# Three of four sums of the heads' outputs, moved one row later in the order of a two-layer attention kernel

## The chip, the cores and the metric

The kernel runs on one core of one Trainium2 chip. The metric is the device time of one execution in microseconds (us); before the change it is 1164.11, the median of three runs (1163.7 to 1166.31). Engines: TensorE (PE; PEld is its loading of stationary operands), VectorE (DVE), ScalarE (ACT), GpSimd (POOL) and SyncE (SP, which here only issues DMAs). Each works through its own queue in the order in which the program issued its instructions, and waits at semaphores for the others.

## The reference, cut to what matters

Two blocks follow one another on x of shape 2 x 1024 x 256 in float32: a one-head causal attention (hidden size 256) with layer norms, and then a second block, which takes most of the time: attention with 16 heads of 128, rotary positions and a causal mask, then a mixture of four experts with two chosen for each token.

```python
q = (h @ wq + bq).reshape(b, s, H, HD)...      # and k, v likewise
q = q * cos + _rotate_half(q) * sin            # and k
scores = jnp.where(causal, jnp.einsum('bhqd,bhkd->bhqk', q, k) / math.sqrt(HD), min)
out = jnp.einsum('bhqk,bhkd->bhqd', softmax(scores), v)
return out.transpose(0, 2, 1, 3).reshape(b, s, H * HD) @ wo + bo
```

The change lies in the second attention: between `out` of two heads and its product with `wo`.

## The kernel before, in words

**Units and rows.** The second attention goes head by head. A pair (g, b) is two heads (group g of 8) of batch element b; 16 pairs make 32 units of one head, and a unit has eight rows i = 0..7, each 128 queries against 128(i+1) keys. `RowB` (line 1123) has the steps of a row: `scores` on TensorE into a score tile of PSUM (two of these exist), then on VectorE `sc` minimum with the causal limit (L617) and the row's maximum (L619); `exponential` on ScalarE (L624); `normalise`, a reciprocal on VectorE (L1158) and a scaling on ScalarE (L1160); `transpose` on VectorE in 32 x 32 blocks (L662), two rows later; `gather`, sixteen DMAs on SP's queue for each four rows in two parts; and `output` on TensorE (L1209), which ScalarE moves into `aT_sb` (L1225). The output of rows 0 to 3 comes eight rows after row 3, that of rows 4 to 7 eight to ten rows after row 7.

**Seven pieces instead of eight.** While a pair's heads are worked through, the projections of the next pair's q and k and of its own v, and the output projection of the pair before, are done with seven half-size products instead of eight (Strassen's scheme in Winograd's form). A projection (`seven_products`, line 899) has pieces p1 to p7, called in the order p1, p2, p4, p3, p6, p5, p7. p2, p5 and p6 end with an addition on VectorE of a PSUM bank and a kept part (`summed`, L952); p7 ends on ScalarE (L944). p1, p3, p5 and p7 add up in one bank "a", so p7's products wait until p5's addition has read that bank. After p2, p6, p5 and p7 a rotation (`rotated`, line 827: two half multiplications L834, one multiplication L835, one addition L836, all on GpSimd) is queued for a later row. All VectorE additions of this kind read one operand from PSUM.

**The sums.** The seven pieces of the output projection (`seven_outputs`, line 1052) need four differences of the finished heads' outputs, `output_sums` (line 1045): each is one subtraction of 128 x 512 floats on VectorE (L1049) with both operands in SBUF.

```python
def output_sums(g, b, n):
    t1, t2, t4 = (scratch[:, ts(k, 512)] for k in range(3))
    b11, b12, b21, b22 = (output_block(g, b, j, k) for j in (1, 2) for k in (1, 2))
    out, in0, in1 = ((t1, b12, b11), (t2, b22, t1), (b12, b22, b12), (t4, b21, t2))[n]
    nc.vector.tensor_tensor(out, in0, in1, ALU.subtract)
```

Sum 0 gives t1, sum 1 t2, sum 2 overwrites b12, sum 3 gives t4. In this profile `scratch` has the name `we_flat`. The pieces are called by block and bank: 11a, 22c (uses t1), 11b, 12+a (t2), 12+c, 22+a (the new b12), 21+a (t4). Each is eight passes on TensorE (L1067) and an addition into `hx` on VectorE (L1076). 11a, 12+a, 22+a and 21+a share bank "a": each of the last three waits for the addition of the one before; 12+c follows 22c in bank "c" in the same way.

**The order.** A planner (`step`, line 1443) writes the calls of each row: scores, fills, exponential, output, mids, transpose of two rows earlier, normalise of one row earlier, gathers, ends, rotations. In the second head of a pair, rows 0 to 2 get two pieces of q each, row 3 gets p7, rows 4 to 6 two output pieces each and row 7 the last; `TS = (1, 2, 2, 3)` (line 1308) puts sum 0 into row 1, sums 1 and 2 into row 2 and sum 3 into row 3. Then `MOVES` (line 28), a list written out by hand, is applied to the names of the calls by `ordered` (line 302): each entry takes a call out and puts it right before another. The program is issued in the order that results; since every engine keeps its queue's order, that list decides what an engine does next. The output sums occur for 14 pairs: (0,0), (1,0), (1,1), (0,1), and (g, b) for g = 2, 3, 4 with both b, then (5,0), (5,1), (6,0), (7,0). They are named by the pair whose outputs are summed.

Of the kernel before, what the change touches and what calls it, by code (L numbers as in the profile page):

```python
# [78 lines left out]
    ("rotation 127", "RowB.normalise 251"),  # L79
    ("wq.7.1 p7", "wo.7.0 11a"),  # L80
    ("RowB.exponential 252", "wq.7.1 p7"),
    ("RowB.scores 252", "RowB.output 243 8"),
    ("RowB.transpose 249", "RowB.scores 252"),
    ("wq.7.1 p5", "RowB.gather 247 1"),
    ("RowB.normalise 250", "RowB.normalise 249"),
    ("rotation 125", "RowB.normalise 250"),
# [14 lines left out]
    ("RowB.gather 239 0", "RowB.normalise 241"),  # L101
    ("RowB.scores 242", "RowB.transpose 239"),
    ("wv.6.1 p3", "RowB.output 231 10"),
    ("wq.6.1 p3", "RowB.output 223 10"),
    ("RowB.normalise 227", "wv.7.0 p6"),
    ("RowB.exponential 227", "RowB.normalise 227"),
    ("RowB.scores 227", "RowB.exponential 227"),
    ("wq.7.0 p7", "weight_sums wv #8"),
    ("RowB.normalise 218", "output_sums 5 1 1"),
    ("RowB.exponential 218", "RowB.normalise 218"),  # L110
    ("wq.7.0 p3", "output_sums 5 1 0"),
    ("wq.7.0 p4", "wq.7.0 p3"),
    ("wv.6.0 p5", "RowB.gather 207 1"),
    ("RowB.scores 210", "RowB.gather 207 0"),
    ("RowB.transpose 202", "wq.6.0 p7"),
    ("RowB.normalise 202", "RowB.transpose 202"),
    ("RowB.transpose 201", "RowB.output 195 8"),
    ("rotation 102", "output_sums 5 0 3"),
    ("rotation 101", "rotation 102"),
    ("wq.6.0 p5", "rotation 101"),  # L120
    ("RowB.gather 199 0", "load_weights 6 wv"),
    ("RowB.transpose 199", "RowB.gather 199 0"),
    ("RowB.normalise 199", "RowB.transpose 199"),
# [1 line left out]
    ("output_weight_sums #7", "wv.5.1 p7"),  # L125
    ("RowB.scores 194", "RowB.gather 191 0"),
    ("wv.5.1 p3", "RowB.exponential 193"),
    ("wq.5.1 p3", "output_sums 4 1 0"),
    ("wq.5.1 p4", "wq.5.1 p3"),
    ("RowB.scores 178", "RowB.gather 175 0"),  # L130
    ("wv.5.0 p3", "RowB.exponential 177"),
    ("wo.4.0 12+a", "RowB.scores 173"),
    ("wo.4.0 11b", "wo.4.0 12+a"),
    ("RowB.exponential 174", "wq.5.0 p5"),
    ("RowB.scores 174", "RowB.exponential 174"),
    ("RowB.transpose 168", "RowB.scores 174"),
    ("rotation 83", "RowB.normalise 167"),
    ("output_weight_sums #6", "RowB.transpose 161"),
    ("RowB.normalise 161", "wv.4.1 p5"),
    ("wq.4.1 p3", "RowB.output 143 10"),  # L140
    ("wv.4.0 p3", "RowB.exponential 145"),
    ("wq.4.0 p3", "RowB.transpose 134"),
    ("wq.4.0 p4", "wq.4.0 p3"),
    ("RowB.normalise 131", "wv.3.1 p6"),
# [2 lines left out]
    ("output_weight_sums #5", "RowB.gather 127 0"),  # L147
    ("RowB.exponential 129", "wv.3.1 p4"),
    ("load_weights 4 wq", "load_weights 3 wo"),
    ("wq.3.1 p5", "RowB.gather 119 1"),  # L150
    ("RowB.exponential 127", "wq.3.1 p5"),
    ("RowB.scores 127", "RowB.exponential 127"),
# [3 lines left out]
    ("RowB.gather 111 1", "RowB.exponential 114"),  # L156
    ("RowB.scores 114", "RowB.transpose 111"),
    ("rotation 55", "wo.2.0 22c"),
    ("wq.3.0 p3", "RowB.output 95 10"),
    ("RowB.transpose 96", "wv.2.1 p5"),  # L160
    ("RowB.scores 98", "RowB.scores 97"),
# [2 lines left out]
    ("wv.2.1 p2", "wv.2.1 p4"),  # L164
    ("wv.2.1 p1", "wv.2.1 p2"),
    ("RowB.gather 91 1", "RowB.normalise 93"),
    ("RowB.transpose 89", "wq.2.1 p7"),
    ("wq.2.1 p5", "RowB.gather 87 1"),
    ("RowB.exponential 91", "wq.2.1 p6"),
    ("RowB.scores 91", "RowB.exponential 91"),  # L170
    ("RowB.scores 82", "RowB.gather 79 0"),
    ("wv.2.0 p3", "RowB.output 71 10"),
    ("RowB.transpose 72", "wq.2.0 p5"),
    ("RowB.exponential 75", "RowB.transpose 72"),
    ("RowB.scores 75", "RowB.exponential 75"),
    ("rotation 35", "RowB.normalise 71"),
    ("wv.0.1 p5", "RowB.gather 63 1"),
    ("wv.0.1 p2", "RowB.exponential 64"),
    ("wo.1.0 11a", "wo.1.0 22c"),
    ("wq.0.1 p7", "wo.1.0 11a"),  # L180
    ("wq.0.1 p5", "output_sums 1 0 3"),
    ("RowB.gather 55 1", "RowB.normalise 57"),
    ("weight_sums wv #2", "RowB.exponential 58"),
    ("RowB.exponential 49", "RowB.normalise 48"),
# [5 lines left out]
    ("RowB.transpose 43", "wo.0.0 12+a"),  # L190
    ("RowB.transpose 42", "wo.0.0 11b"),
    ("rotation 22", "weight_sums wk #2"),
    ("output_sums 0 0 3", "wq.1.1 p6"),
    ("output_sums 0 0 1", "RowB.scores 42"),
    ("RowB.transpose 39", "RowB.output 31 10"),
    ("RowB.transpose 38", "RowB.transpose 39"),
    ("wq.1.1 p4", "RowB.scores 41"),
# [1719 lines left out]
```

## Time and profile before

| | |
|---|---|
| time, median of 3 runs | 1164.11 us (1163.7 to 1166.31) |
| profiled execution: time, span from first to last instruction | 1165.19 us, 1163.4 us |
| mean granted TensorE clock | 0.994 |
| busy: PE, DVE, POOL, ACT | 1133.0, 852.5, 789.5, 648.7 us |
| L1049, output sums on VectorE | 56 instructions: 25.3 + 24.0 + 17.7 us busy |
| L952, the queries' additions (Twq) | 30 + 15 instructions, mean 680 and 678 ns |
| L1076, the output pieces' additions (hx) | 70 + 28 instructions, mean 680 and 682 ns |
| L834, L835, L836, rotations on GpSimd | means 1309/1300, 1341/1298, 1336/1281 ns |

A row of the profile's groups names the line, the engine, the operation, what it writes and reads, the count and the mean; a row of the timeline begins with the start and the duration in us. Numbers after `<-` in brackets are idle time of that engine and who ended it. The end of a matmul is modelled: a record of TensorE lasts longer than the distance to the next one's start, so the time that TensorE loses is read from the distances of starts.

### The profile page before, as it was taken

Reading aid. Unit: us, or ns where it says so; the run is one execution under the profiler, and the core shown is the slowest. Engines: PE = TensorE matmul, PEld = TensorE weight load, DVE = VectorE, ACT = ScalarE, POOL = GpSimd, SP = SyncE. Lnnn points to the kernel's source line nnn. Section 1 sums busy time; section 2 is a strip of 40 time slices with the busy share of each in tenths; the row PEclk is TensorE's granted clock in tenths of the full one; section 3 lists DMA queues with packets and bytes.
Section 4 is the critical chain, followed back from the end, with each engine's and each line's share of the span. In section 5 each row is a group of like instructions: output and inputs, shape, how many; then the busy total and the mean of one; then the engine's idle time right before and its main releaser. Section 6 shows DMA issues by size and latency. Waiting matters only on the chain.

```text
span 1163.4 us, 15802 instructions
## 1 busy us (share of the span) xinstructions
PE 1133.0 (97%) x4628; PEld 718.6 (62%) x4628; DVE 852.5 (73%) x1813; ACT 648.7 (56%) x1228; POOL 789.5 (68%) x749
## 2 busy tenths in 40 slices
PE   8999989999999999999999999999999999999997
PEld 5666636656565656565757475756566656566765
DVE  5667797868686868687877778777868677575675
ACT  3333676665656565656566656565565656553444
POOL 4005999989897979697878868797989897002100
PEclk9999999999999999999999999999999999899999
DMA  6132465665546454555555545564555657405011
GB/s 187 36 88 57 117 174 140 135 138 125 127 113 130 107 138 110 118 122 131 119 125 131 131 112 131 132 138 115 132 129 128 148 121 180 106 15 145 1 37 36
DMA packets 243221, 133.89 MB, mean 115 GB/s; under 512 B 18908, under 2 KB 241184, under 8 KB 242368
## 3 DMA queue, kind: packets, MB, share of 16 engines
q1 hardware_dynamic: 238096, 123.02, 45.6%
q0 software_dynamic: 1776, 4.89, 1.6%
q10 hardware_dynamic: 3264, 4.98, 1.2%
q8 instruction: 37, 0.61, 0.2%
q14 instruction: 48, 0.39, 0.1%
HBM read 22.71 MB, written 4.19 MB: 23 GB/s over the span
## 4 chain that ended last, share of the span: by engine, by line
PE 87%; DVE 8%; DMA 2%; issue 1%; SPq 1%; ACT 1%; POOL 0%; DVEq 0%; ACTq 0%; POOLq 0%
PE sc L1143 19%; PE av L1209 19%; PE pa L919 10%; PE pa L1067 5%; PE pa L910 5%; PE pa L1685 5%; PE pe L1708 4%; PE pc L919 4%; PE pa L741 2%; PE sc L692 2%; PE pc L1067 2%; PE pc L910 2%; PE pa L599 1%; PE pa L586 1%; PE pa L1019 1%
## 5 line engine op out<-in xcount | busy, mean ns | idle before, releaser
L1160 ACT ACTIVATE pr<-pr,rs 128x128 f32<-128x128 f32 (+3 forms) x252 | 195.6, 778 | 188.9 <-DVE rs L1158 188.9
L1143 PE MATMUL sc<-Twk,Twq 128*128 128x512 f32 (+3 forms) x768 | 289.5, 487 | 4.3 <-ACT pr L624 4.3
L624 ACT ACTIVATE pr<-sc,nmx 128x640 f32<-128x640 f32 (+7 forms) x272 | 200.9, 739 | 154.4 <-DVE nmx L619 121.6
L1209 PE MATMUL av<-pT,vg 128*128 128x512 f32 (+3 forms) x768 | 271.0, 490 | 4.7 <-DMA pT<-pair_sb 2.4
L834 POOL TENSOR_TENSOR rot<-Twk,rope_sb 64x512 f32<-64x512 f32 x128 | 167.6, 1309 | 92.2 <-DVE Twk L952 70.0
L1209 PEld LDWEIGHTS av<-pT,vg 128*128 128x128 f32 x768 | 143.5, 191 | 128.6 <-issue 99.3
L619 DVE TENSOR_REDUCE nmx<-sc 128x1 f32<-128x640 f32 (+7 forms) x272 | 206.1, 758 | 9.4
L1143 PEld LDWEIGHTS sc<-Twk,Twq 128*128 128x128 f32 x768 | 135.6, 191 | 123.9 <-issue 108.7
L834 POOL TENSOR_TENSOR rot<-Twq,rope_sb 64x512 f32<-64x512 f32 x128 | 166.3, 1300 | 8.8
L617 DVE TENSOR_TENSOR sc<-sc,limit 128x128 f32<-128x128 f32 x272 | 79.2, 291 | 99.6 <-PE sc L1143 84.0
L662 DVE STREAM_TRANSPOSE x<-pr 128x640 f32<-128x640 f32 (+1 forms) x124 | 128.4, 1036 | 19.6 <-ACT pr L1160 11.9
L835 POOL TENSOR_TENSOR Twk<-Twk,rope_sb 128x512 f32<-128x512 f32 x64 | 85.8, 1341 | 5.0
L836 POOL TENSOR_TENSOR Twk<-Twk,rot 128x512 f32<-128x512 f32 x64 | 85.5, 1336 | 5.0
L835 POOL TENSOR_TENSOR Twq<-Twq,rope_sb 128x512 f32<-128x512 f32 x64 | 83.1, 1298 | 5.0
L836 POOL TENSOR_TENSOR Twq<-Twq,rot 128x512 f32<-128x512 f32 x64 | 82.0, 1281 | 5.0
L1577 POOL TENSOR_TENSOR hx<-hx,x 128x256 f32<-128x256 f32 x16 | 11.5, 745 | 90.1 <-DVE hx L1717 82.7
L662 DVE STREAM_TRANSPOSE pair_sb<-pr 128x128 f32<-128x128 f32 (+1 forms) x120 | 60.2, 502 | 8.0 <-ACT pr L1160 7.8
L1685 PE MATMUL pa<-xT,we_flat 128*128 128x512 f32 x128 | 59.6, 611 | 0.8 <-DVE hx L1029 0.8
L1076 DVE TENSOR_TENSOR hx<-hx,pa 128x512 f32<-128x512 f32 x70 | 46.6, 680 | 13.6 <-PE pa L1067 13.5
L1225 ACT ACTIVATE aT_sb<-av,par 128x512 f32<-128x512 f32 x64 | 43.8, 684 | 21.3 <-PE av L1209 19.8
L1708 PE MATMUL pe<-lent,hT 128*128 128x256 f32 x240 | 54.2, 379 | 0.0
L624 ACT ACTIVATION_READ_ACCUMULATOR pr<-sc,nmx 128x1 f32 x272 | 53.4, 196 | 0.0
(215 smaller groups left out, 1810.5 us busy)
## 6 DMA issues: line engine op xcount, KB each, us to landing
pT<-x SPq DMA_DIRECT2D x496, 128.0 KB, 2.7
pT<-pair_sb SPq DMA_DIRECT2D x480, 64.0 KB, 2.0
pT<-aT_sb SPq DMA_DIRECT2D x48, 128.0 KB, 2.7
pT<-za SPq DMA_DIRECT2D x48, 64.0 KB, 2.1
wk_g<-in_L_ffn_wk_dram SPq DMA_DIRECT2D x9, 256.0 KB, 3.0
wq_g<-in_L_ffn_wq_dram SPq DMA_DIRECT2D x9, 256.0 KB, 3.1
wv_g<-in_L_ffn_wv_dram SPq DMA_DIRECT2D x9, 256.0 KB, 3.1
wo_g<-in_L_ffn_wo_dram SPq DMA_DIRECT2D x9, 256.0 KB, 2.9
```

Of the source, the lines that this page charges most:

```text
L619: nc.vector.tensor_reduce(nmx, sc[:, :L], AX.X, ALU.max, negate=True)
L624: nc.scalar.activation(pr[:, :L], sc[:, :L], AF.Exp, bias=nmx, accum_out=sm)
L662: nc.vector.transpose(z[:, i % 4, :n, :], pr[:, : n * 32].rearrange("p (m s) -> p m s", s=32))
L834: nc.gpsimd.tensor_tensor(rot[lo, :], t[hi, cs], rope_sb[hi, 1, cs], ALU.mult)
L835: eng.tensor_tensor(t[:, cs], t[:, cs], rope_sb[:, 0, cs], ALU.mult)
L836: nc.gpsimd.tensor_tensor(t[:, cs], t[:, cs], rot, ALU.add)
L919: nc.tensor.matmul(pa, lhsT=w, rhs=x, start=start, stop=True, skip_group_check=True)
L1143: nc.tensor.matmul(sc[:, ds(n0, n)], lhsT=qT[:, ts(i, P)], rhs=kT[:, ds(n0, n)], start=True, stop=True,)
L1160: nc.scalar.activation(self.pr[:, :L], self.pr[:, :L], AF.Copy, scale=rs)
L1209: nc.tensor.matmul(cut(av), lhsT=vg[g, b][:, c, ts(hh, HD)], rhs=cut(pT[:, c, :]), start=(c == 0), stop=(c == i),)
L1685: nc.tensor.matmul(ph, lhsT=we1_sb[:, e, c, ts(m, P)], rhs=x2T[:, c, ds(k0 * P, 512)], start=(c == 0), stop=(c == DC - 1),)
L1708: nc.tensor.matmul(pe[:, ts(n, D)], lhsT=hTs[b, j, e][:, c, ts(k, P)], rhs=we2_sb[e][:, c, :], start=(c == 0), stop=(c == IC - 1),)
```

## The change

The list of moves gets new entries. Sums 1 and 2 go from row 2 of the second head to row 3, right behind the row's scores, minimum and maximum; sum 3 goes from row 3 to row 4, at the same place in it. Sum 0 stays. Other new or altered entries only keep the calls around the sums where they were, since old entries had used a sum as their mark. What is computed is the same. The lines removed and added, in order:

```diff
-    ("RowB.scores 252", "RowB.output 243 8"),
+    ("RowB.scores 252", "output_sums 7 0 3"),
...
+    ("RowB.exponential 251", "RowB.transpose 249"),
+    ("output_sums 7 0 2", "RowB.exponential 251"),
+    ("output_sums 7 0 1", "output_sums 7 0 2"),
...
+    ("output_sums 6 0 3", "weight_sums wv #9"),
+    ("output_sums 6 0 2", "RowB.exponential 235"),
+    ("output_sums 6 0 1", "output_sums 6 0 2"),
...
-    ("RowB.normalise 218", "output_sums 5 1 1"),
+    ("output_sums 5 1 3", "wq.7.0 p7"),
+    ("output_sums 5 1 2", "RowB.exponential 219"),
+    ("output_sums 5 1 1", "output_sums 5 1 2"),
+    ("RowB.normalise 218", "wq.7.0 p6"),
...
+    ("output_sums 5 0 3", "weight_sums wv #7"),
...
-    ("rotation 102", "output_sums 5 0 3"),
+    ("rotation 102", "RowB.exponential 203"),
...
+    ("output_sums 5 0 2", "wq.6.0 p5"),
+    ("output_sums 5 0 1", "output_sums 5 0 2"),
...
+    ("output_sums 4 1 3", "wo.4.1 11a"),
+    ("output_sums 4 1 2", "RowB.exponential 187"),
+    ("output_sums 4 1 1", "output_sums 4 1 2"),
...
+    ("output_sums 4 0 3", "weight_sums wv #6"),
+    ("output_sums 4 0 2", "RowB.exponential 171"),
+    ("output_sums 4 0 1", "output_sums 4 0 2"),
...
+    ("output_sums 3 1 3", "wo.3.1 11a"),
+    ("output_sums 3 1 2", "RowB.exponential 155"),
+    ("output_sums 3 1 1", "output_sums 3 1 2"),
...
+    ("output_sums 3 0 3", "weight_sums wv #5"),
+    ("output_sums 3 0 2", "RowB.exponential 139"),
+    ("output_sums 3 0 1", "output_sums 3 0 2"),
...
+    ("output_sums 2 1 3", "wo.2.1 11a"),
+    ("output_sums 2 1 2", "RowB.exponential 123"),
+    ("output_sums 2 1 1", "output_sums 2 1 2"),
...
+    ("output_sums 2 0 3", "weight_sums wv #4"),
+    ("output_sums 2 0 2", "RowB.exponential 107"),
+    ("output_sums 2 0 1", "output_sums 2 0 2"),
...
+    ("output_sums 0 1 3", "wo.0.1 11a"),
...
-    ("RowB.scores 91", "RowB.exponential 91"),
+    ("RowB.scores 91", "output_sums 0 1 1"),
...
+    ("output_sums 1 1 3", "weight_sums wv #3"),
...
-    ("RowB.scores 75", "RowB.exponential 75"),
+    ("RowB.scores 75", "output_sums 1 1 1"),
+    ("RowB.exponential 74", "RowB.scores 75"),
+    ("wq.2.0 p6", "RowB.exponential 74"),
...
-    ("wq.0.1 p5", "output_sums 1 0 3"),
+    ("output_sums 1 0 3", "weight_sums wk #3"),
+    ("wq.0.1 p5", "RowB.exponential 59"),
+    ("output_sums 1 0 2", "wq.0.1 p5"),
+    ("output_sums 1 0 1", "output_sums 1 0 2"),
...
-    ("output_sums 0 0 3", "wq.1.1 p6"),
-    ("output_sums 0 0 1", "RowB.scores 42"),
+    ("output_sums 0 0 3", "wo.0.0 11a"),
+    ("output_sums 0 0 2", "RowB.exponential 43"),
+    ("output_sums 0 0 1", "output_sums 0 0 2"),
```

## The prediction

> **What bounds the kernel now.** I read the page first, then busy time in the stretch that the change touches, then the waits, then the rows of the moved sums, and last the timelines of one place. The page's engine shares and its chain:
>
> ```profile
> PE 1133.0 (97%) x4628; PEld 718.6 (62%) x4628; DVE 852.5 (73%) x1813; ACT 648.7 (56%) x1228; POOL 789.5 (68%) x749
> ...
> PE 87%; DVE 8%; DMA 2%; issue 1%; SPq 1%; ACT 1%; POOL 0%; DVEq 0%; ACTq 0%; POOLq 0%
> ```
>
> TensorE carries the chain. The windows view of 190 to 930 us, which holds thirteen of the fourteen places that change (the last lies at 944):
>
> ```profile
> 190.00:930.00 740.00, 734.09 (x3091) 457.79 (x3090) 563.79 (x1105) 443.42 (x843) 628.77 (x586) 1.00 0.55 127
> ```
>
> PE busy comes first: 5.9 us of 740 idle, at a granted clock of 1.00. Only TensorE's own waits can be won. The waits view of the same stretch has them:
>
> ```profile
> PEld pa L919 <- DVE Twq L952: 8.1, 12, 1.6
> ...
> PE pa L919 <- DVE Twq L952: 5.9, 7, 1.4
> ```
>
> Both are one wait: the queries' last piece p7 adds into the bank that p5's addition (L952, on VectorE) must first have read. In TensorE's timeline a 512-column pass starts every 0.43 us; what p7's first pass loses beyond its pitch is, by place (named by the pair whose outputs are summed): (0,0) 0.88, (1,0) 0.88, (1,1) 1.52, (0,1) 1.62, (2,0) 0.41, (2,1) 0.14, (3,0) 0.13, (3,1) 0.14, (4,0) 0.19, (4,1) 0.13, (5,0) 1.34, (5,1) 0.41, (6,0) 0.14, (7,0) none: 7.9 us. After each wait p7's second pass starts 0.10 late too: 13 x 0.10 = 1.3. So 9.3 us at most (more than the idle time, since a pass's record, 0.59, is longer than its pitch). The moved sums themselves, by their line:
>
> ```profile
> L1049 DVE TENSOR_TENSOR we_flat<-aT_sb,we_flat x28: 681/820/1751, 210.3 to 952.1; 128x512 f32<-128x512 f32 x28
> L1049 DVE TENSOR_TENSOR we_flat<-aT_sb x14: 681/1266/1567, 198.9 to 944.1; 128x512 f32<-128x512 f32 x14
> L1049 DVE TENSOR_TENSOR aT_sb<-aT_sb x14: 1298/1750/1756, 212.1 to 948.0; 128x512 f32<-128x512 f32 x14
> ```
>
> One shape takes from 681 to 1756 ns. Why, the timelines of VectorE and of GpSimd at (3,1) show:
>
> ```profile
> 606.34 0.56 DVE L619 TENSOR_REDUCE nmx<-sc 128x1 f32<-128x384 f32 x1
> 606.81 0.93 DVE L1049 TENSOR_TENSOR we_flat<-aT_sb,we_flat 128x512 f32<-128x512 f32 x1
> 607.66 1.75 DVE L1049 TENSOR_TENSOR aT_sb<-aT_sb 128x512 f32<-128x512 f32 x1
> 609.34 0.68 DVE L952 TENSOR_TENSOR Twq<-pc,part 128x512 f32<-128x512 f32 x1
> 609.94 0.68 DVE L952 TENSOR_TENSOR Twq<-pa,part 128x512 f32<-128x512 f32 x1
> ...
> 611.72 0.72 DVE L1049 TENSOR_TENSOR we_flat<-aT_sb,we_flat 128x512 f32<-128x512 f32 x1
> ...
> 613.99 0.68 DVE L1076 TENSOR_TENSOR hx<-hx,pa 128x512 f32<-128x512 f32 x1
> ```
>
> ```profile
> 607.27 1.60 POOL L835 TENSOR_TENSOR Twk<-Twk,rope_sb 128x512 f32<-128x512 f32 x1
> 608.95 1.60 POOL L836 TENSOR_TENSOR Twk<-Twk,rot 128x512 f32<-128x512 f32 x1
> 610.63 2.94 POOL L834 TENSOR_TENSOR rot<-Twq,rope_sb 64x512 f32<-64x512 f32 x2
> ```
>
> Sums 1 and 2 (606.81, 607.66) stand ahead of the additions of p6 and p5 (609.34, 609.94), whose pieces were done by 607.68. A sum ends 0.55 us after the GpSimd operation that it met: sum 2 at 609.41, that operation at 608.87. GpSimd's next one then takes 1.60 instead of 1.27. Sum 3 (611.72) met the last 0.17 us of an operation and took 0.72.
>
> **The change, part by part.** Applying both lists of moves to the sequence of calls, only the 42 sums change place; no instruction is added, no DMA moves. Sums 1 and 2 go behind the minimum and maximum of row i=3, sum 3 behind those of row i=4. Ahead of p5's addition they are gone at (0,0), (2,0) to (4,1), (5,1), (6,0) and (7,0), not at (1,0), (1,1), (5,0), where p5 follows row 3's scores, nor at (0,1), where both p6 and p5 do. Behind them now stand the transpose of row 1 and reciprocal of row 2, and behind sum 3 all four additions of the outputs' pieces (L1076); TensorE waits for those: 12+a for 11a's, 22+a for 12+a's, 21+a for 22+a's. In the trace these have 2.02, 1.50 and 2.40 us to spare, but at (0,0) 22+a has 0.44; at (2,1) 21+a has 0.69; at (4,0) 12+a has 0.93; at (5,1) 12+a has 1.19 and 22+a 0.96.
>
> What a sum costs at its new place no row shows. Bounds: 0.68 (no operation met) and 1.75 (a whole one). I take the end of the operation that it will meet plus 0.55. This is where a rule weighs against the change. The row: sum 3 took 0.68 to 0.72 at thirteen places, and at that price nine places just lose their waits. The Trainium skill, page "SBUF — State Buffer", section "Who interferes with whom", says that a VectorE instruction with two SBUF inputs and a GpSimd instruction that reads SBUF exclude each other, whoever starts first keeping the port to its end. Then 0.72 belongs to the old place, not to the sum. The rows of 1.75 behind another sum agree, so I follow the rule.
>
> Worked at (3,1); VectorE starts the next instruction some 0.08 before the last one's end. p6's addition at 606.87, p5's at 607.71 (its piece ends 607.68), transpose and reciprocal 0.27, row 3's minimum 0.30 and maximum 0.61 from 608.58: sum 1 starts at 609.49. GpSimd, undisturbed, runs 607.27 to 608.54 and 608.62 to 609.89 (1.27 each): sum 1 ends 610.44, the operation behind it takes 1.60 to 611.57, sum 2 ends 612.12. Transpose and reciprocal 0.42; row 4's scores end at 612.63 on a TensorE that is 0.24 ahead, so its minimum starts 612.66 (before 612.91) and sum 3 at 613.70. It meets an operation that ends at 614.60: 1.45 us. 11a's addition starts 615.07 (before 613.99); 12+a has 0.68 left. 12+a's addition ends 619.27; 22+a stands at 619.72: 0.45 left. By the addition of 21+a, where VectorE was idle for 1.05, it has caught up. Gain 0.24. Covers: ScalarE's exponential of row 3 comes earlier (609.6, before 611.9), that of row 4 as before; row 3's transpose, hence its gather on SP, is about 1.2 later, but is read eight rows on, over 20 us away, and its sixteen DMA issues take some 11 us. GpSimd is delayed by as many sums as before. Without the cover of those 0.45 us every late microsecond of VectorE is one of TensorE.
>
> The other places in the same way, minus is gain:
> - (3,0), (3,1), (4,1), (6,0): 0.23 + 0.24 + 0.24 + 0.24 = -0.95.
> - (2,0): -0.52, with 0.1 left at 22+a.
> - (0,0): -0.98; 12+a's addition ends 225.5 (before 225.2) with TensorE 0.98 ahead and 0.44 to spare: 22+a waits 0.88 + 0.10. Net 0.
> - (2,1): -0.24; sum 3 ends at 506.3, 11a's addition at 506.9, 12+a stands there at 506.64: +0.36; 22+a +0.25; 21+a +0.6. Net +1.0.
> - (5,1): -0.52; sum 3 ends 841.0, so 12+a waits 0.8 and 22+a 0.24. Net +0.5.
> - (4,0): -0.30 against +0.37 at 12+a, about 0. (7,0): no wait before, 0.8 left after, 0.
> - p5 still behind: (1,0) -0.43 and (1,1) -0.14, since the sums meet shorter remainders there; (0,1) +0.5, since sum 1 meets a longer one (1.5 instead of 1.09); (5,0): sum 1 and a GpSimd operation are ready at the same time, 776.17: -0.34 or +0.92, taken at +0.3.
>
> Sum: -0.95 - 0.52 + 1.0 + 0.5 - 0.43 - 0.14 + 0.5 + 0.3 = +0.3 us. On the profiled execution (1165.19; span 1163.4 and 1.8 around it) that makes 1165.5; it ran 1.08 above the median, 1164.11, so I predict 1164.4. The bounds: with every sum at 0.68 the nine freed places give -3.5, and at the other four VectorE saves 1.3 to 1.8 ahead of p5, which takes (1,0) -0.98, (1,1) and (0,1) -1.48 each, (5,0) -1.33: -8.8. With every sum at 1.75 it is +8.5 (rival b at all its places).
>
> **The rivals.**
> (a) The sums keep their prices, sum 3 at 0.72: nine waits vanish and nothing takes their place. 0.98 + 0.52 + 0.24 + 0.23 + 0.24 + 0.30 + 0.24 + 0.52 + 0.24 = 3.5: 1160.6. For it: VectorE is only 76% busy in the stretch (563.79 of 740), and its idle time grows when it needn't hold TensorE. Against: the spread of the sums' rows.
> (b) Slower: VectorE's backlog lands on the outputs' additions. If sum 1 meets a whole operation too (1.75 instead of 0.95) and sum 3 as well (1.75 instead of 1.45), 11a's addition comes 1.1 later still: at (3,1) 12+a then waits 1.1 - 0.68 = 0.42 and 0.10, and 22+a 1.1 - 0.52 - 0.45 = 0.13 and 0.10, in all 0.75 on top of my value. At half of the eleven places other than (1,0), (1,1), (7,0) that is +4.1, with my +0.3: 1168.5. It decides from the point where these additions come over 1.5 us later against TensorE than before. For it: GpSimd runs without a pause there (gaps of 0.08), and (0,0), (2,1), (4,0), (5,1) have less to spare. Against: a sum's mean meeting is half an operation.
> (c) The sums meet no operation of GpSimd: -8.8, so 1155.3. Against it: GpSimd's timeline has no gap for them, and sum 2, straight behind sum 1, took 1.75 at all but one place.
>
> **How the numbers follow.** Chances: the exchange 0.44 (own range 1162 to 1166.5), (a) 0.26 (1158.5 to 1161.8), (b) 0.27 (1166.5 to 1172), (c) 0.03. About 0.2% (2.3 us) is what a measurement can tell from no change. Of the exchange 0.40 lies within it and 0.02 at either side; (a) and (c) add 0.29 below, (b) 0.27 above: faster 0.31, same 0.40, slower 0.29. The range for 8 in 10 runs from 1159 to 1170; it leaves out (c) and the outer parts of (a) and (b).
>
> **What would show it.** Right: L919's wait for L952 under 0.1 at the regular places, but still over 0.4 at (1,0), (1,1), (0,1), (5,0); sum 3 mostly at 1.2 to 1.75 us; new waits of TensorE at L1067 for "DVE hx" at (0,0), (2,1), (5,1), together 2 to 4 us. Wrong towards (a): no such rows and a sum 3 near 0.7. Wrong towards (b): L1067 waits at most places. What would upset the working most is the phase of GpSimd's operations, which sets each sum's length and which I carried on from the old trace.

## The result

The changed kernel took 1166.37 us (median of 22 runs, 1162.96 to 1171.09), the kernel before 1163.21 us in the same set of runs (22, 1159.25 to 1166.95). The ratio is 1.0031, 95% interval [1.0019, 1.0042]: slower by 3.6 us, where +0.3 was predicted as the likeliest. The time lies inside the range, but on the far side of the 0.2% that I took for no change.

The profiled execution of after doesn't show this loss: 1165.7 us, span 1163.1, at a clock of 0.996 (before: 1165.19, 1163.4, 0.994). One profile is one draw: before's has one stretch more at half clock, behind a wait for a gather near 933 us. So the time is taken apart in two ways: TensorE's records of after and before (4628 each, in the same order), aligned one to one, give what each place gains or loses; the mean granted clock of all timed runs gives the rest. From after's page:

```profile
PE 1130.3 (97%) x4628; PEld 717.3 (62%) x4628; DVE 861.8 (74%) x1813; ACT 652.6 (56%) x1228; POOL 790.8 (68%) x749
```

VectorE is busy 9.3 us more for the same 1813 instructions. The line of the sums (L1087, before L1049) says where (minimum, median, maximum in ns):

```profile
L1087 DVE TENSOR_TENSOR we_flat<-aT_sb,we_flat x28: 681/1410/1741, 214.0 to 952.4; 128x512 f32<-128x512 f32 x28
```

This row holds sums 1 and 3; its median went from 820 to 1410. Sum 3 alone took 0.68 to 0.72 at thirteen places before and now takes 1.39 to 1.74 at twelve of fourteen. TensorE's own waits from 190 to 930 us (engine, line, whom it waited for; total us, times, longest):

```profile
PE pa L957 <- DVE Twq L990: 5.4, 4, 2.1
PE sc L1181 <- ACT pr L662: 0.9, 1, 0.9
PE pa L1105 <- DVE rs L1196: 0.6, 1, 0.6
PE pa L1105 <- DVE hx L1114: 0.6, 1, 0.6
```

Before, one row stood here: 5.9 us in 7 waits for p5's addition. Four are left, and they are longer (2.1 instead of 1.4); the three rows below are new. By place (what TensorE loses or wins there in all, in us; minus is gain):

| place | predicted | measured | what is seen in after |
|---|---|---|---|
| (3,0), (3,1), (4,1), (6,0) | -0.95 | -0.93 | no wait left |
| (2,0) | -0.52 | -0.51 | no wait left |
| (1,0), (1,1) | -0.57 | -0.57 | p7 waits 0.45, 1.38 |
| (0,0) | 0 | +0.11 | p7's wait gone, 0.3 at 12+a, 0.8 at 22+a |
| (0,1) | +0.5 | +0.41 | p7 waits 2.02 |
| (5,1) | +0.5 | +0.54 | 0.8 at 12+a, 0.2 at 22+a |
| (2,1) | +1.0 | +1.34 | 0.3 at 12+a, 1.2 at the scores |
| (4,0) | 0 | +0.29 | 0.2 at 11a, 0.4 at 12+a |
| (5,0) | +0.3 | +0.91 | p7 waits 2.25 |
| (7,0) | 0 | 0.00 | none within the place |
| sum | +0.26 | +1.59 | |

These 1.59 us are at full clock. The rest goes with the clock: the timed runs of after have a mean granted clock of 0.9946 (standard error 0.0003), those of before 0.9961, 0.9962, 0.9968 and 0.9973 in four later sets of runs; before's clock in the set of the result itself isn't on record. 0.001 of the clock is 1.2 us if TensorE is busy all the while (1160 us x 0.001). Over the 144 runs of before the span falls by 0.9 us for each 0.001, over after's 22 by 1.2. So a clock that is lower by 0.0015 to 0.0027 stands for 1.3 to 3.1 us. Together 2.9 to 4.7, against 3.6 [2.2, 4.9] measured. In the records, a stretch of reduced clock is 3.4 or 6.8 us at one half, so at most 1.7 or 3.4 us are lost. The stretch that ends every run (1.5 to 4.6 us of it within the span) finds TensorE idle: it counts in the mean clock and costs no time. Span times clock, roughly a run's time at full clock, has a mean of 1158.67 us in after, of 1157.18 in the 70 runs of before in the first two sets of experiments and of 1156.92 in all 144: +1.5 to +1.75, which agrees with the +1.59 of the aligned records.

**The worked place, (3,1).** VectorE and GpSimd in after:

```profile
607.84 0.69 DVE L990 TENSOR_TENSOR Twq<-pa,part 128x512 f32<-128x512 f32 x1 [0.17 <-PE pa L957]
...
609.63 0.87 DVE L1087 TENSOR_TENSOR we_flat<-aT_sb,we_flat 128x512 f32<-128x512 f32 x1
...
613.80 1.40 DVE L1087 TENSOR_TENSOR we_flat<-aT_sb,we_flat 128x512 f32<-128x512 f32 x1
615.12 0.68 DVE L1114 TENSOR_TENSOR hx<-hx,pa 128x512 f32<-128x512 f32 x1
```

```profile
608.68 1.27 POOL L874 TENSOR_TENSOR Twk<-Twk,rot 128x512 f32<-128x512 f32 x1
...
613.38 1.27 POOL L873 TENSOR_TENSOR Twq<-Twq,rope_sb 128x512 f32<-128x512 f32 x1
```

p5's addition now waits for TensorE (0.17) instead of TensorE for it. Sum 1 ends at 610.50, 0.55 after the GpSimd operation it met (609.95); sum 3 at 615.20, 0.55 after its one (614.65). The forecast had 610.44, and 615.15 for sum 3; 11a's addition was put at 615.07 and started at 615.12. The wait of p7 left and the sums paid for it on VectorE, as worked. The same holds far beyond this place: in all fourteen profiles (before, after and the twelve experiments) 780 of the 784 sums last 0.68 us or the rest of the GpSimd operation that they meet plus 0.55, whichever is longer, to 0.01 us; the other four are told in the last section.

### The profile page after: what moved, and what is told of

It is laid out like the page before. It is cut to its first block, busy times and chain, and to the rows that moved or that the text cites. A ratio compares the mean times of both kernels' runs of the same rounds, so it can differ in the third digit from the quotient of the medians.

```text
span 1163.1 us, 15808 instructions
## 1 busy us (share of the span) xinstructions
PE 1130.3 (97%) x4628; PEld 717.3 (62%) x4628; DVE 861.8 (74%) x1813; ACT 652.6 (56%) x1228; POOL 790.8 (68%) x749
## 4 chain that ended last, share of the span: by engine, by line
PE 85%; DVE 9%; DMA 3%; SPq 2%; issue 1%; ACT 0%; ACTq 0%; DVEq 0%
PE av L1247 19%; PE sc L1181 18%; PE pa L957 10%; PE pa L948 5%; PE pa L1723 5%; PE pa L1105 5%; PE pe L1746 4%; PE pc L957 4%; PE sc L730 2%; PE pc L948 2%; PE pa L779 2%; PE pc L1105 2%; SPq L711 2%; DMA pT<-x 2%; DVE we_flat L1087 1%; DVE nmx L657 1%
## 5 line engine op out<-in xcount | busy, mean ns | idle before, releaser
L1181 PE MATMUL sc<-Twk,Twq 128*128 128x512 f32 (+3 forms) x768 | 289.7, 487 | 5.3 <-ACT pr L662 5.3
L1181 PEld LDWEIGHTS sc<-Twk,Twq 128*128 128x128 f32 x768 | 135.6, 191 | 125.1 <-issue 109.3
L872 POOL TENSOR_TENSOR rot<-Twq,rope_sb 64x512 f32<-64x512 f32 x128 | 171.4, 1339 | 8.8
L874 POOL TENSOR_TENSOR Twk<-Twk,rot 128x512 f32<-128x512 f32 x64 | 82.5, 1289 | 5.0
L873 POOL TENSOR_TENSOR Twk<-Twk,rope_sb 128x512 f32<-128x512 f32 x64 | 82.0, 1281 | 5.0
```

What stands on the lines that cost most here:

```text
L872: nc.gpsimd.tensor_tensor(rot[lo, :], t[hi, cs], rope_sb[hi, 1, cs], ALU.mult)
L873: eng.tensor_tensor(t[:, cs], t[:, cs], rope_sb[:, 0, cs], ALU.mult)
L874: nc.gpsimd.tensor_tensor(t[:, cs], t[:, cs], rot, ALU.add)
L1181: nc.tensor.matmul(sc[:, ds(n0, n)], lhsT=qT[:, ts(i, P)], rhs=kT[:, ds(n0, n)], start=True, stop=True,)
```

## The experiments

**Theory.** An exchange, place by place: a sum is as long as what is left of the GpSimd operation it meets, plus 0.55 us. Where sums 1 and 2 are put behind p5's addition, p7's wait goes; where they stay ahead of it, it may grow; sum 3 in row 4 delays the output pieces' additions. **Rival A** for the rest of the loss: the two long waits, 2.0 us at (0,1) and 2.2 at (5,0), lower the clock. **Rival B**: the late stretch behind (7,0), where TensorE waits for gathers, does. A third possibility was that the exchange isn't what decides, but the mere length of the sums.

The edits are entries at the end of the list of moves, so each is shown by its pattern. "Clock" is the mean of the timed runs of the kernel, minus that of before in the same set of runs, with a standard error of 0.0004 to 0.0006 (0.0007 to 0.0009 where only five or six runs were timed); 0.001 is about 1 us.

| kernel | ratio [95%] | sum of places, us | clock, minus before's |
|---|---|---|---|
| seven places | 0.9985 [0.9975, 0.9996] | -2.0 | +0.0005 |
| four places | 1.0052 [1.0038, 1.0067] | +3.2 | -0.0016 |
| sum 3 late | 0.9990 [0.9978, 1.0002] | -1.85 | -0.0010 |
| p5 first | 0.9986 [0.9975, 0.9997] | -3.7 | -0.0018 |
| (7,0) alone | 1.0011 [0.9999, 1.0022] | +0.4 | -0.0012 |
| (0,1) and (5,0) alone | 1.0005 [0.9993, 1.0017] | +1.35 | +0.0004 |
| both, without (7,0) | 0.9910 [0.9891, 0.9928] | -8.03 | +0.0011 |
| both, with (7,0) | 0.9908 [0.9888, 0.9928] | -8.03 | +0.0013 |
| change without (7,0) | 1.0004 [0.9991, 1.0018] | +1.37 | +0.0002 |
| (7,0), sum 3 alone | 0.9999 [0.9986, 1.0011] | 0.0 | 0.0000 |
| (7,0), sums 1 and 2 alone | 1.0023 [1.0013, 1.0032] | +1.1 | -0.0012 |
| change, experts' loads late | 1.0040 [1.0025, 1.0056] | +1.63 | -0.0025 |

"Sum of places" leaves out the time lost to half clock inside a place (2.58 - 0.9 = 1.7 us at (5,0) in one profile, about as much at (0,1) in another).

**1. The change only where a gain was worked out.** On the kernel before:

```diff
+    ("output_sums 3 1 1", "RowB.exponential 155"),
+    ("output_sums 3 1 2", "RowB.exponential 155"),
+    ("output_sums 3 1 3", "wo.3.1 11a"),
...
```

and so at (1,0), (1,1), (2,0), (3,0), (4,1), (6,0).

> The change at seven places only: (1,0), (1,1), (2,0), (3,0), (3,1), (4,1), (6,0). Theory (the waits for p5 are exchanged, place by place, for sums that meet GpSimd operations and for waits of the outputs' pieces): these seven are the gaining ones, TensorE ends each of them earlier by 0.43, 0.14, 0.51 and four times 0.23, in all 2.0 us, as in the trace of the whole change; about 1161 us, ratio 0.998. Rival (the loss comes from later gathers behind the late transposes, whichever place is changed): TensorE's DMA waits behind the places grow and the ratio is above 1.

Measured 0.9985, -1.7 us; the seven places gave -0.41, -0.14, -0.51, -0.22, -0.24, -0.23, -0.24. **2. Only where a loss was worked out**, in the same way at (0,1), (2,1), (5,0), (5,1).

> The change at four places only: (0,1), (2,1), (5,0), (5,1). Theory: these lose, by 0.41, 1.34, 0.90 and 0.54, in all 3.2 us, so about 1166.4, ratio 1.003, as much as the whole change loses in its timed runs. Rival (the loss lies at the DMA waits near 990 us, made by the last places (6,0) and (7,0), which are unchanged here): no loss, 1163.

Measured 1.0052, +6 us in 5 runs, nearly twice what was expected; the places lost 0.43, 1.35, 0.9 and 0.53 at full clock, 3.2 in all. The rest goes with a lower clock (-0.0016, standard error 0.0008), here with (7,0) untouched; the profile has one stretch of half clock behind the wait at (5,0). So the change is a mixture of places with both signs, and at full clock its places add up: what each loses or gains alone, it does in the whole.

**3. Sum 3 later.** On the changed kernel, sum 3 at all fourteen places behind the addition of 22+a:

```diff
+    ("output_sums 3 1 3", "RowB.transpose 156"),
...
```

> The whole change, but sum 3 of all 14 places goes two rows later still, behind the addition of 22+a in row 6 (only 21+a in row 7 reads it). Theory: sum 3's 1.4 to 1.7 us ahead of 11a's addition is what makes 12+a and 22+a wait; moved behind them, (2,1), (5,1), (0,0) and (4,0) lose no time there, about 3 us under the whole change: 1163, unless 21+a at (2,1), where row 7 has no scores, waits up to 1 us. Rival (the sums 1 and 2 alone fill VectorE): the waits of 12+a and 22+a stay, 1166.

Measured 0.9990. (0,0) went from +0.11 to -0.84, (2,1) from +1.34 to +0.35, (4,0) from +0.29 to -0.13, (5,1) from +0.54 to -0.51, which are the places where sum 3 had eaten the slack of the output pieces. (0,1) and (5,0) stayed (2.08, of which some 1.7 half clock, and 0.90).

**4. Sums behind p5.** On the changed kernel, sums 1 and 2 behind p5's addition where that stands behind row 3's scores:

```diff
+    ("output_sums 1 0 1", "RowB.exponential 59"),
+    ("output_sums 1 0 2", "RowB.exponential 59"),
+    ("output_sums 1 1 1", "RowB.normalise 73"),
+    ("output_sums 1 1 2", "RowB.normalise 73"),
+    ("output_sums 0 1 1", "RowB.gather 87 1"),
+    ("output_sums 0 1 2", "RowB.gather 87 1"),
+    ("output_sums 5 0 1", "rotation 101"),
+    ("output_sums 5 0 2", "rotation 101"),
```

> The whole change, but at (1,0), (1,1), (0,1) and (5,0) sums 1 and 2 stand behind p5's addition instead of ahead of it. Theory: p7's waits there (0.45, 1.38, 2.02, 2.25 and 0.10 after each) go, 6.5 us under the whole change if the outputs' pieces there have the slack that the other places have, about 1160. Rival (VectorE's backlog only moves on): 12+a and 22+a wait there instead, at least half is given back, 1163 or more.

Measured 0.9986: (1,0) -0.57, (1,1) -1.62, (0,1) -1.68, (5,0) -0.62, where the change had -0.43, -0.14, +0.41, +0.91. VectorE's timeline at (5,0) in after:

```profile
776.13 1.72 DVE L1087 TENSOR_TENSOR we_flat<-aT_sb,we_flat 128x512 f32<-128x512 f32 x1
777.77 1.75 DVE L1087 TENSOR_TENSOR aT_sb<-aT_sb 128x512 f32<-128x512 f32 x1
779.44 0.68 DVE L990 TENSOR_TENSOR Twq<-pa,part 128x512 f32<-128x512 f32 x1
```

and GpSimd's at the same time:

```profile
776.04 1.27 POOL L874 TENSOR_TENSOR Twk<-Twk,rot 128x512 f32<-128x512 f32 x1
```

GpSimd started at 776.04, sum 1 at 776.13: 0.09 us too late, so it had a whole operation ahead of it, and p5's addition stood behind 3.3 us of sums. It fell so in all six profiles that have this order, by 0.08 to 0.11 us.

**5 and 6. Rivals A and B alone.** On the kernel before, the change only at (7,0), and only at (0,1) and (5,0):

```diff
+    ("output_sums 7 0 1", "RowB.exponential 251"),
+    ("output_sums 7 0 2", "RowB.exponential 251"),
+    ("output_sums 7 0 3", "RowB.output 243 8"),
```

```diff
+    ("output_sums 0 1 1", "RowB.exponential 91"),
+    ("output_sums 0 1 2", "RowB.exponential 91"),
+    ("output_sums 0 1 3", "wo.0.1 11a"),
+    ("output_sums 5 0 1", "wq.6.0 p5"),
+    ("output_sums 5 0 2", "wq.6.0 p5"),
+    ("output_sums 5 0 3", "weight_sums wv #7"),
```

> The change at (7,0) only. So far the places' own losses explain 1.6 us of the whole change, its timed runs lose over 3, and they show a lower granted clock (mean 0.9946 against 0.9967 before; one less in a thousand is 2.3 us at half clock and 1.2 us lost). Theory A (the clock drops after the long waits for p5, which are above 2 us at (0,1) and (5,0) only): here no place loses and the clock is as before, 1162.8 us, ratio 1.000, clock 0.997. Theory B (the clock drops at the gather waits near 933 and 990 us, which the last place (7,0) alone can disturb): clock 0.995 and 2 to 3 us more, ratio 1.002.

> The change at (0,1) and (5,0) only, where sums 1 and 2 stay ahead of p5. The places themselves lose 0.4 + 0.9 = 1.3 us. Theory A (waits over 2 us for p5 drop the clock): besides, the clock is lower in the mean, 0.995, and the time is some 3.5 us above before, ratio 1.003. Theory B (the gather waits behind (7,0) drop it): clock 0.997, 1.3 us more, ratio 1.001.

(7,0) alone: 1.0011, with an interval that just includes no change, and a clock lower by 0.0012 (1.1 to 1.4 us), though its records hold only a wait of 0.3 us and its echo of 0.1 at 955 us. (0,1) and (5,0) alone: 1.35 us of places and a clock as before. A falls as the main cause: its waits were there and the clock was not lower. It isn't nothing. Six profiles hold those two waits, and in two of them half clock follows one. The windows around (5,0) in the kernel of experiment 2 (start and end, length, busy us of PE, PEld, DVE, ACT, POOL, granted clock, DMA share, GB/s):

```profile
779.93:783.34 3.41, 1.32 (x6) 0.65 (x5) 2.73 (x5) 1.28 (x2) 3.27 (x3) 1.00 0.97 258
783.34:786.75 3.41, 3.41 (x12) 2.38 (x11) 1.71 (x4) 0.71 (x2) 3.25 (x3) 0.50 1.16 208
```

and in after, where the wait was as long (2.25 us):

```profile
778.63:782.04 3.41, 1.87 (x5) 0.91 (x6) 2.47 (x5) 1.45 (x3) 3.22 (x3) 1.00 0.97 262
```

The window behind this one ran at 1.00. Why these windows are cut as they are, and why the same wait weighs so differently, is told in the last section.

**7 and 8. Both cures.** Sums 1 and 2 in row 3, nowhere ahead of p5, and sum 3 behind 22+a's addition, at thirteen places and at all fourteen; (3,1) and (5,0) for example:

```diff
+    ("output_sums 3 1 1", "RowB.exponential 155"),
+    ("output_sums 3 1 2", "RowB.exponential 155"),
+    ("output_sums 3 1 3", "RowB.transpose 156"),
...
+    ("output_sums 5 0 1", "rotation 101"),
+    ("output_sums 5 0 2", "rotation 101"),
+    ("output_sums 5 0 3", "RowB.transpose 204"),
```

> Thirteen places, without (7,0): sums 1 and 2 in row 3 but nowhere ahead of p5's addition, sum 3 behind the addition of 22+a in row 6. Theory (exchange): no wait for p5 is left and the outputs' pieces wait for nothing but a part of 21+a at (2,1): of the 9.3 us of waits in the trace of before about 7.5 are won; with the clock as before 1155 us, ratio 0.9935. Rival (backlog): 21+a or the next unit's scores wait for sum 3 at most places, ratio above 0.997. Theory B of the clock expects 0.997 here, theory A as well.

> The same with (7,0) as well. Theory A of the clock (long waits for p5): as without (7,0), 1155 us, clock 0.997. Theory B (the gather waits behind (7,0)): clock 0.995, some 2 us more than without (7,0).

1152.4 and 1152.04 us (six runs each), ratios 0.9910 and 0.9908: faster than both kernels, and than the 1155 expected. The places gave 8.0 us; a clock higher by 0.0011 and 0.0013 is about 1.3 us more. Of 735 us, TensorE is idle for 0.25 (the first figure behind the length is its busy time) in the kernel without (7,0):

```profile
185.00:920.00 735.00, 734.75 (x3109) 459.32 (x3108) 570.79 (x1110) 448.78 (x847) 632.91 (x589) 1.00 0.56 129
```

VectorE is as busy there as in after (570.79 of 735 us; 570.83 of 740): the long sums are still long. They only stand where nothing waits. The third possibility falls with that. What was expected of theory B fell here too: with (7,0) the clock was no lower than without, and three of six runs of each reached 0.998. At (7,0) this kernel has sums 1 and 2 in row 3 as the change has, and only sum 3 later.

**9 and 10. What of (7,0) lowers the clock.** The change at the other thirteen places; and on the kernel before, sum 3 of (7,0) alone:

```diff
+    ("output_sums 7 0 3", "RowB.output 243 8"),
```

> The change at thirteen places, with (7,0) left as before. The exchange at the places is that of the whole change, +1.6 us, and (7,0) has no part in it. Theory B (the rest of the loss, 1.5 to 2 us of half clock per run, comes from the late stretch behind (7,0), which the moved sums of (7,0) shift against its gathers): the half-clock time falls from 12.5 to about 8 us per run, mean clock 0.9965, ratio 1.001 to 1.0015. Theory A (it comes from the long waits for p5's addition at (0,1) and (5,0), 2.0 and 2.2 us): those waits are still there, so clock 0.9946 and ratio 1.003 as with the whole change.

> The kernel before with sum 3 of (7,0) alone one row later, sums 1 and 2 where they were. No TensorE wait is there to win or lose at (7,0): at full clock within 0.3 us of before. Theory B, in the form that sum 3 behind row 4 is what shifts the late stretch: mean clock 0.995, half-clock time 11 to 12 us per run, ratio 1.001 as with all three sums of (7,0). Theory A, or chance in the earlier run: clock 0.9965, half clock 8 us per run, ratio 1.000.

Without (7,0) the ratio fell from 1.0031 to 1.0004 and the clock was that of before, although the waits of A were all there: as B had it, if a little lower than its 1.001. Sum 3 alone did nothing. **11. Sums 1 and 2 of (7,0) alone** (t4 is formed there ahead of its t2, so the outputs of that pair of heads aren't the reference's, and only the time counts):

```diff
+    ("output_sums 7 0 1", "RowB.exponential 251"),
+    ("output_sums 7 0 2", "RowB.exponential 251"),
```

> The kernel before with sums 1 and 2 of (7,0) alone in row 3, sum 3 where it was. All three together kept every run of three kernels under a mean clock of 0.998 and made TensorE wait 2.7 to 3.8 us near 990 us for the last gather; sum 3 alone did neither. Theory B1 (sums 1 and 2 do it, by delaying the transpose and the gather of row 3, so that the next loads and gather stand one behind the other on SP): no run at or over 0.998, clock 0.995, wait near 990 us over 2.5 us, ratio 1.001. Theory B2 (only all three together): about a third of the runs at or over 0.998, clock 0.9965, wait 1.0 to 1.6 us, ratio 1.000.

1.0023: 1.1 us of its own (three sums in a row ahead of 11a's addition; the records show a wait of 1.0) and 1.1 to 1.4 us of clock. B1, but not as sharply: 4 of 22 runs reached 0.998, against 17 of 31 of before. In the kernels with all three sums moved in the change's way at (7,0) (after, experiments 4, 5, 12) none of 59 runs did; of before 50 of 144; with sum 3 behind 22+a at (7,0) (experiments 3 and 8) 7 of 28. As far as these counts go, neither part alone does it in full: it takes sums 1 and 2 in row 3 with sum 3 close to them. TensorE's wait for the gather `pT<-x` near 990 us goes with it: before, then after:

```profile
PE av L1209 <- DMA pT<-x: 2.3, 1, 2.3
```

```profile
PE av L1247 <- DMA pT<-x: 4.5, 1, 4.5
```

Counted beyond the pitch of the passes, this wait is 3.8 in after, 3.2, 2.7, 3.2 and 4.2 in experiments 4, 5, 11, 12; it is 1.6 in before and 0.9 to 2.4 in the other eight. What is late there shows in SP's queue, before and then after:

```profile
959.54 10.82 SPq L673 DMA_DIRECT2D pT<-pair_sb  x16
...
971.57 0.58 SPq L1507 DMA_DIRECT2D wgate_sb<-in_L_ffn_w_gate_dram  x1
973.03 11.27 SPq L673 DMA_DIRECT2D pT<-x  x16
```

```profile
958.85 10.91 SPq L711 DMA_DIRECT2D pT<-pair_sb  x16
...
970.97 0.58 SPq L1545 DMA_DIRECT2D wgate_sb<-in_L_ffn_w_gate_dram  x1
971.66 12.11 SPq L711 DMA_DIRECT2D pT<-x  x16
```

TensorE of after reaches this gather's data 1.46 us earlier than in before, which has lost 1.7 us to half clock at 934 us. The first gather starts only 0.69 earlier, so 0.77 late against TensorE. The loads of the experts' weights behind it are late too, and the second gather stands right behind them. It starts only 0.09 late against TensorE, but takes 12.11 us to issue instead of 11.27, and TensorE goes on 7.6 us after its last issue instead of 6.4 (at 991.4). In sum TensorE waits 2.2 us longer. Some of it comes back at once: before then waits another 0.8 us for `hx`, after does not.

Over the fourteen profiles the issue of this gather goes with the change at (7,0): 11.7 to 13.4 us in after and experiments 4, 5, 11 and 12 (in the last with other loads between its halves), 10.8 to 11.4 in the nine others. The time from the last issue does not: 6.0 to 7.6 against 5.7 to 7.5, so that a part of after's long wait may belong to this one execution. Nor is the first gather always late: against TensorE by 0.77 to 1.33 us in after and experiments 4, 5 and 12, by nothing in experiment 11, which still waits 3.2. So the delay that B1 named is not what makes the wait there.

**12. The experts' loads behind that gather**, on the changed kernel:

```diff
+    ("load_experts", "RowB.scores 258"),
```

> The whole change, with the loads of the experts' first weights and of the router's (1,028 KB, issued on SP straight ahead of the last gather but one of the scores) issued behind that gather. If the gather lands late because it shares the DMA engines with these loads, the wait near 990 us falls from 3.8 to under 1.6 us, the half-clock time from 12.5 to 8 us per run or less, a third or more of the runs reach a clock of 0.998, and the ratio falls from 1.003 to 1.001. If it is late because it is issued late on SP or for another reason, the wait stays over 2.5 us and the ratio at 1.003. The places' exchange of +1.6 us stays in both.

It did not help: 1.0040, wait 4.2 us, no run at 0.998. The loads didn't go behind the gather on SP but between its two halves (eight issues at 973.8, the loads at 979.1, eight at 980.4), so half of it still stood behind them. Whether the loads make this gather late isn't settled, then.

## Why the prediction was right or wrong

- **The lock as the price of a sum: right.** Rest of the GpSimd operation plus 0.55 us, and 1.60 instead of 1.27 for what follows when GpSimd comes second. To follow the rule that the Trainium skill has on page "SBUF — State Buffer", section "Who interferes with whom", against the row of 0.72 was the right choice: rival (a) expected a sum 3 near 0.7, and it is 1.39 to 1.74 at twelve places. Eleven places came within 0.12 us of their working, (0,0) by parts that weren't worked (0.3 at 12+a).
- **(5,0): the other of two outcomes.** I named -0.34 or +0.92 and took +0.3; it was +0.91. A mean of two outcomes can't happen, and it was no toss from run to run: six of six profiles fell the same way. 0.6 us of the miss.
- **(2,1): right in direction, short in what waits.** I let 12+a, 22+a and 21+a wait. In the trace 12+a does (0.3), the other two don't; the larger part, 1.07 us and 0.10 behind it, is at the next scores (L1181), for row 4's exponential, which started when VectorE had done row 3's reciprocal at 506.97, behind sum 3 and two additions. I had followed the additions and not ScalarE. 0.34 us. The waits at (0,0), (2,1) and (5,1) come to 3.7 us, within the 2 to 4 that I named as a sign, but only a part of them is for `hx`.
- **(4,0): 0 against +0.29.** 12+a waits 0.41, where I had 0.37; p7's gain is 0.29. What was missed is 0.17 at 11a, for ScalarE's end of p7.
- **(7,0): 0, the step that failed most.** "row 3's transpose, hence its gather on SP, is about 1.2 later, but is read eight rows on, over 20 us away": true of that gather, and at thirteen places all there is to say, but I didn't follow SP's queue behind it. At (7,0) the loads for the experts and one more gather stand there, and that gather already made TensorE wait 1.6 us in before. With the same change left out at (7,0), the clock was as before and the ratio 1.0004. That the moved sums there lower the clock is shown by experiments 5, 9 and 11 together, and by the counts (none of 59 runs at 0.998, against a third); that it goes by way of the gather's longer wait is read from the profiles, with the rule of the last section, and no run took that wait away by itself.
- **The clock wasn't in the sum at all.** I costed waits at their length. Behind some of them TensorE runs 3.4 or 6.8 us at half speed. A stretch of 3.4 cost 1.7 us more in the aligned records (before near 934 us, experiments 2 and 3), nearly as much again as the wait. The profile of before already showed it, a granted clock of 0.63 from 934 to 938 us, behind a wait for a gather.
- **Rival (b)** has the right sign and, with 1168.5, about the right distance, but not its mechanism: the places cost 1.6 us, where it had 4.4; output pieces wait at the four places that I had named as short of time, and at no other.
- **The number.** The range held the time, the likeliest value did not. Of the 3.3 us between +0.3 and +3.6, 1.3 are the places, nearly all of it (5,0), (2,1) and (4,0); the larger part goes with the clock, for which I had no term. The range was wide enough for it because of the rivals, not because I had foreseen it. (The bound of 9.3 us on what the waits for p5 can give is 9.2 by its own terms; nothing rests on it.)

What stays open: what makes the gather near 990 us take longer to issue, and whether its wait is what lowers the clock. Before's own mean clock moved from 0.9961 to 0.9973 between sets of runs, so a difference of 0.001 means something only within one set, and there it is about two standard errors.

## What to carry to other kernels

When an instruction moves away from a wait, look up what stands behind it at the new place, on its own engine and on each queue that its followers feed, to the end of that queue: here the same long sums cost +3.6 us in one position and saved 11 us (with rows 3 and 6) in another. A VectorE instruction that shares a lock with GpSimd has no fixed length; if two possible meetings differ by less than 0.1 us, forecast both. And a TensorE wait of over 1.8 us can cost more than its length, in some executions or in all, as the next section works out.

## What the runs showed of the hardware

The granted clock goes by windows on a fixed grid. In the twelve of fourteen profiles that have more than one half-clock stretch, their starts lie whole multiples of 3.413 us apart (in before: 933.57, 991.60, 1158.85, that is 17.0 and 49.0 windows), and each lasts one window or two, but for the last, which the end of the run cuts. Laying this grid over TensorE's records shows what decides, as far as fourteen profiles can: all 34 stretches come right behind a window in which TensorE was busy for 46% or less, and of the windows from 5 us on that full clock followed five lay at 45 or 46% and none lower. The edge is narrow: between 1.53 and 1.58 us of busy time in 3.41 four windows brought half clock and five did not, which is as fine as these modelled records go; below, all did, above, none. Experiment 3 at (0,1), 1.56 us busy, half clock next:

```profile
382.89:386.30 3.41, 1.56 (x7) 0.95 (x7) 2.90 (x6) 1.25 (x4) 3.27 (x3) 1.00 0.87 199
386.30:389.71 3.41, 3.41 (x9) 1.86 (x8) 0.64 (x3) 1.59 (x3) 3.17 (x4) 0.50 0.88 196
```

and experiment 6 at the same place, 1.57 us busy, full clock:

```profile
384.22:387.63 3.41, 1.57 (x8) 1.07 (x7) 3.13 (x6) 0.88 (x3) 3.27 (x3) 1.00 0.83 188
387.63:391.05 3.42, 3.42 (x21) 2.46 (x21) 1.86 (x5) 2.08 (x5) 3.25 (x3) 1.00 0.88 199
```

A second half-clock window followed where TensorE was busy for 63 to 76% of the first (six cases), and none where it was 86% or more (14). The grid lies differently against the program in each execution. From the edge at 46%: a wait with under 1.84 us of idle time would not lower the clock by itself; one of 2 us does so when it falls into one window, as in experiment 2 at (5,0), and not when a window's border splits it, as in after; and one over 3.7 us leaves one window under 46% wherever the border falls. Near 990 us TensorE is idle for 2.3 us in before and for 4.5 in after: the first can be split by a border, the second is too long for that, which fits that no run of after came near full clock (0.997 at most) while a third of before's reached 0.998. The Trainium skill, page "TensorE: Matmul & The Clock Gate", section "Part 1: The HAM clock gate", has the free-running window of some 3.4 us, and says that an idle window brings the half clock; here a window that was busy for 46% was idle enough.

Who goes first between VectorE and GpSimd is decided within some hundredths of a microsecond. Where a sum started 0.001 to 0.011 us behind a GpSimd operation (sum 1 at (4,0) in experiments 3, 7, 8 and 9, the four exceptions to the rule above), the sum still took 0.68 us and the GpSimd operation 1.80 instead of 1.27. Where it started 0.061 us or more behind, it waited for the whole rest.
